# The opening of a four-layer kernel: order of the first loads, and a ternary rounding shared with GpSimd

## Chip, core and metric

One Trainium2 chip; the kernel runs on one of its cores. The metric is the device time of one execution in microseconds, here the median of three runs. Engines are named as the profile names them: PE (TensorE), DVE (VectorE), ACT (ScalarE), POOL (GpSimd), SP (SyncE).

## What is computed

Four conditioned layers one after the other on x of 64 sequences, 64 tokens and 256 features, in float32. Only the first is touched by the change, and only in its opening:

```python
def _L0_cond_ref(x, cond, norm_w, up_w, down_w):
    def act_quant(x):
        scale = 127.0 / jnp.clip(jnp.max(jnp.abs(x), axis=-1, keepdims=True), 1e-05, None)
        return jnp.clip(jnp.round(x * scale), -128.0, 127.0) / scale
    def weight_quant(w):
        scale = 1.0 / jnp.clip(jnp.mean(jnp.abs(w)), 1e-05, None)
        return jnp.clip(jnp.round(w * scale), -1.0, 1.0) / scale
    scale = cond @ norm_w.T + 1.0
    ms = jnp.mean(x * x, axis=-1, keepdims=True)
    h = x * (scale[:, None, :] * jax.lax.rsqrt(ms + EPS))
    u = h @ up_w.T
    val, gate = jnp.split(u, 2, axis=-1)
    h = val * jax.nn.gelu(gate, approximate=False)
    hq = h + jax.lax.stop_gradient(act_quant(h) - h)
    wq = down_w + jax.lax.stop_gradient(weight_quant(down_w) - down_w)
    return hq @ wq.T + x
```

The other layers are an attention block with a gated feed-forward part (L1), a layer norm (L2) and a bottleneck whose weights are generated per sequence (L3): `dWd = (h_lang @ Wdd.T + bdd) * 0.1`, and the like for `dWu`.

## The kernel before

The 4096 tokens are worked in 8 blocks of 512, a block in 4 tiles of 128 tokens. For layer 0 the function `l0` runs 32 tiles n. A tile's two `upper` halves multiply x, scaled by the condition and split in two fp32r parts (`xh`, `xl`), by the up weights, split likewise, in three passes (`mm3`, L83 to L85); ACT turns the gate into `g` with Gelu and the row scale `rs` (L433), DVE multiplies into `h` (L434). `quant` (L440 to L447) finds the row maximum on DVE, rounds `h` to `q`, and lets SP issue a transposing DMA to `qt`. `lower(n)`, some tiles later, multiplies `qt` by the ternary down weights `wq` (L459) and adds x.

The opening, before the loop, is written out by hand, and each engine keeps to its order there, SP too. Inside the loop PE, ACT, DVE and POOL keep to program order, while SP's order comes from a scheduler. All DMAs of a queue are issued in its order, and a DMA whose buffer or completion counter is not free holds up those behind it.

The up weights come in four pieces j of 512 columns, `ups[j]`, in the order of need: piece 2 (gate) and 0 (value) for the first half of the tiles, 3 (gate) and 1 (value) for the second. `load_up(j, queue, chunks)` (L321) loads one; `half_hi` (L327, ACT) casts it to the high part and `half_lo` (L330, DVE) subtracts for the low part. Pieces 2 and 0 come over ACT's queue, 3 and 1 over SP's. `prep_load(i)` (L361) loads a block of x feature-major (`xf`) and token-major (`xt`); for block 0 it loads only the first half of `xf`, and `rest_load` (L374) the other half, `xt` and pieces 3 and 1. `prep_parts` (L387) scales and splits x; `prep_scale` (L401) takes four square sums of `xt` on ACT (L219) and the root `rs` on POOL (L210, L212). `first((0, 1))` (L404) multiplies the first halves of tiles 0 and 1 chunk by chunk, in 24 products (L415), and does the Gelu later. `warm` (L465) issues transposes of the identity before the data is there.

The ternary rounding of the down weights `wd` (two tiles of 4 x 256 columns in one buffer of eight) is in three parts: `ternary_load`, `ternary` (two absolute sums on ACT, L346) and `ternary_rest` (L348), which, after tile 2, sums over partitions on PE, takes the reciprocal in `sb`, and rounds in three instructions a tile on DVE, L357 to L359.

A guard copy is a one-column POOL copy into a load's target that reads an earlier load's data; it holds the load until that data is there. Before, they stand at L339 (wd, until piece 3), L380 (piece 3, until `cwn`, the condition weights), L274 (the first four `gt`, until `xt`) and L134 (`cwt`, until `gl`). `gt` are tiles of the weight generator's matrix: `gen_load` (L266), `gen_make` (L278, the products L285), `gen_stage` (L289, ACT copies) and `gen_store` (L303); the first four are worked at tile 5. `cond_load` (L128) loads `vc`, `bo` and `cwt` for the other condition vectors, which are computed at tile 6.

Of the kernel before, what the change touches and what calls it, by code (L numbers as in the profile page):

```python
# [8 lines left out]
F32 = mybir.dt.float32  # L9
F32R = mybir.dt.float32r  # L10
BF16 = mybir.dt.bfloat16
AF = mybir.ActivationFunctionType
ALU = mybir.AluOpType
# [4 lines left out]
P = 128  # L18
NB = 64
L = 64  # L20
D = 256
NTOK = NB * L
T = 512
NBLK = NTOK // T
BB = T // L
# [4 lines left out]
MAGIC = 12582912.0  # L30


V_NORM, V_AG, V_AB, V_AA, V_FG, V_FB, V_FA, V_LIN = range(8)
# [3 lines left out]
def tile_kernel(ctx: ExitStack, tc, xT, x, condT, cw, upT, downT, qkvT, woT, ghT, outT_w,  # L37
                vecs, rows, g1, g2, gb, out):
    nc = tc.nc
# [12 lines left out]
    pools = {}  # L52
# [24 lines left out]
    def tok(ap, i):  # L77

        return ap[i * T:(i + 1) * T, :].rearrange("(t p) d -> p t d", p=P)
# [7 lines left out]
    def b3(ap):  # L87
        return ap.rearrange("p (b l) -> p b l", l=L)
# [23 lines left out]
    def bc(v, c, i, bs=slice(0, BB)):  # L112

        n = bs.stop - bs.start
        return cv[:, v, c, i * BB + bs.start:i * BB + bs.stop].unsqueeze(2).broadcast_to([P, n, L])
# [10 lines left out]
    crest = {}  # L126

    def cond_load():  # L128
        nc.sync.dma_start(out=vc, in_=vecs)
        bo = crest["bo"] = pools["a"].tile([NB, D], F32, name="bo")  # L130
        nc.sync.dma_start(out=bo, in_=rows[0:1, :].broadcast_to([NB, D]))

        cwt = crest["w"] = pools["kv"].tile([P, TT, 2, 8, 32], F32, tag="vb", bufs=2, name="cwt")[:, :2].rearrange("p a e h d -> p (a e) (h d)")
        nc.gpsimd.tensor_copy(cwt[:, 0, 0:1], gl[:, 0:1])  # L134
        nc.sync.dma_start(out=cwt[0:64], in_=cw[:, 1:5, :])
        nc.sync.dma_start(out=cwt[64:128, 0:3], in_=cw[:, 5:8, :])
# [173 lines left out]
    def l0(hooks):  # L310
# [10 lines left out]
        def load_up(j, queue, chunks=slice(0, 2)):  # L321
            if j not in ups:
                ups[j] = main.tile([P, 2, 512], F32, tag="x1", bufs=X1, name=f"upst{j}")
            queue.dma_start(out=ups[j][:, chunks],
                            in_=upT.rearrange("(c p) n -> p c n", p=P)[:, chunks, j * 512:(j + 1) * 512])
# [4 lines left out]
        def half_lo(j, c):  # L330
            js = slice(j * 512, (j + 1) * 512)
            nc.vector.tensor_tensor(up[1][:, c, js], ups[j][:, c], up[0][:, c, js].bitcast(F32), ALU.subtract)

        def ternary_load():
            wd = pools["kv"].tile([P, 8, D], F32, tag="kb", bufs=2, name="wd")
            til["wd"] = [wd[:, 4 * j:4 * j + 4] for j in range(2)]

            for j in range(2):
                nc.gpsimd.tensor_copy(wd[:, 4 * j, 0:1], ups[3][:, j, 0:1])  # L339
            for j in range(2):  # L340
                nc.sync.dma_start(out=til["wd"][j], in_=downT.rearrange("(f p) d -> p f d", p=P)[:, 4 * j:4 * j + 4, :])

        def ternary():
            for j in range(2):
                wj = main.tile([P, 4, D], F32, tag="xn", bufs=1, name=f"wj{j}")
                nc.scalar.activation(wj, til["wd"][j], AF.Abs, accum_out=sa[:, j:j + 1])  # L346

        def ternary_rest():  # L348
            wd, ones = til.pop("wd"), til.pop("ones")
            pb = bank("mm")  # L350
            nc.tensor.matmul(pb[:, 0:2], lhsT=ones, rhs=sa, start=True, stop=True)
            nc.vector.tensor_reduce(sb[:, 0:1], pb[:, 0:2], AX.X, ALU.add)
            nc.vector.tensor_scalar(sb[:, 1:2], sb[:, 0:1], 1.0 / (FF * D), 1e-5, ALU.mult, ALU.max)
            nc.vector.reciprocal(sb[:, 2:3], sb[:, 1:2])
            for j in range(2):
                wj = main.tile([P, 4, D], F32, tag="xn", bufs=1, name=f"wk{j}")
                nc.vector.tensor_scalar(wj, wd[j], sb[:, 2:3], MAGIC, ALU.mult, ALU.add)  # L357
                nc.vector.tensor_scalar(wj, wj, -MAGIC, 1.0, ALU.add, ALU.min)
                nc.vector.tensor_scalar(wq[:, 4 * j:4 * j + 4, :], wj, -1.0, None, ALU.max)  # L359

        def prep_load(i):  # L361
            xf = pool.tile([P, 2, T], F32, tag="xf", bufs=1, name=f"xf{i}")
            xt = None if i == 0 else block(f"xt{i}")
            xfs[i] = xf
            blk[i] = [xt, None, parts(f"l0_{i}"), None]
            src = xT.rearrange("(c p) t -> p c t", p=P)[:, :, i * T:(i + 1) * T]
            if i == 0:

                nc.sync.dma_start(out=xf[:, :, :T // 2], in_=src[:, :, :T // 2])
            else:  # L370
                nc.sync.dma_start(out=xf, in_=src)
                nc.sync.dma_start(out=xt, in_=tok(x, i))

        def rest_load():  # L374

            xf = xfs[0]
            ups[3] = main.tile([P, 2, 512], F32, tag="x1", bufs=X1, name="upst3")
            ups[1] = main.tile([P, 2, 512], F32, tag="x1", bufs=X1, name="upst1")
            xt = blk[0][0] = block("xt0")
            nc.gpsimd.tensor_copy(ups[3][0:64, 0, 0:1], cwn[:, 0:1])  # L380
            load_up(3, nc.sync)
            load_up(1, nc.sync)
            nc.sync.dma_start(out=xt, in_=tok(x, 0))
            nc.sync.dma_start(out=xf[:, :, T // 2:], in_=xT.rearrange("(c p) t -> p c t", p=P)[:, :, T // 2:T])
            nc.sync.dma_start(out=ct[64:128], in_=condT)

        def prep_parts(i, bs=slice(0, BB)):  # L387

            xf, hl = xfs[i], blk[i][2]
            ts = slice(bs.start * L, bs.stop * L)  # L390
            xss = []
            for c in range(2):
                xs = main.tile([P, T], F32, tag="xg", bufs=2, name=f"xs{i}_{c}_{bs.start}")[:, ts]
                nc.vector.tensor_tensor(b3(xs), b3(xf[:, c, ts]), bc(V_NORM, c, i, bs), ALU.mult)
                xss.append(xs)
            for c in range(2):
                yield
                nc.scalar.copy(hl[0][:, c, ts], xss[c])
                nc.vector.tensor_tensor(hl[1][:, c, ts], xss[c], hl[0][:, c, ts].bitcast(F32), ALU.subtract)

        def prep_scale(i):  # L401
            blk[i][1] = rms(blk[i][0], f"l0_{i}")
# [65 lines left out]
            for _ in range(n):  # L468
                nc.tensor.transpose(pb[:, :P], ident, ident)

        for c in range(2):
            load_up(2, nc.scalar, slice(c, c + 1))
        prep_load(0)
        til["ones"] = pool.tile([P, P], F32, name="ones")

        nc.scalar.activation(sa, nhalf[:, 0:2], AF.Gelu)
        nc.gpsimd.memset(til["ones"], 1.0)
        for c in range(2):
            load_up(0, nc.scalar, slice(c, c + 1))
        rest_load()  # L480
# [2 lines left out]
        cond_norm()  # L483
        warm(10)

        for c, _ in enumerate(prep_parts(0, slice(0, BB // 2))):
            if c == 1:
                half_hi(2, 1)
            half_lo(2, c)
        for c in range(2):  # L490
            half_hi(0, c)
            half_lo(0, c)
        first((0, 1))
        for j in (3, 1):
            for c in range(2):
                half_hi(j, c)
                half_lo(j, c)
        prep_scale(0)
        for _ in prep_parts(0, slice(BB // 2, BB)):
            pass  # L500
        upper(0, 0, "rest")
# [7 lines left out]
        for n in range(N + 2):  # L509
            if n < N:  # L510
                if n > 1:
                    upper(n, 0)
                if n == 0:
                    ternary_load()
                if n in visits:
                    for _ in range(4):
                        gen_make()
                        gen_stage()
                for _ in range(0 if n == 4 else 2 if n in visits and (n + 3 in visits or n == visits[-1]) else 1):
                    gen_load(blk[0][0][:, n, 0:1] if n < 4 else None)  # L520
                    gen_store()
                upper(n, 1)
                if n == 1:
                    ternary()
                    blk[0][3] = block("x1_0")
                if n == 2:
                    ternary_rest()
                if n % TT == 0 and n // TT + 1 < NBLK:
                    prep_load(n // TT + 1)
                if n % TT == 1 and n // TT + 1 < NBLK:  # L530
                    for _ in prep_parts(n // TT + 1):
                        pass
                if n % TT == 2 and n // TT + 1 < NBLK:
                    prep_scale(n // TT + 1)
            if n == N - 1:
                quant(n)
            for hook in hooks.get(n, ()):
                hook()
            if n < N - 1:
                quant(n)  # L540

            if n > 3:
                for k in range({4: 0, N + 1: N - 1}.get(n, n - 3), {N: N - 1, N + 1: N}.get(n, n - 2)):
                    lower(k)
# [695 lines left out]
```

## Time and profile before

| | |
|---|---|
| median of three runs | 763.72 us (763.22 to 764.21) |
| profiled execution | 762.64 us |
| its span, first to last instruction | 760.9 us |
| mean granted TensorE clock | 0.999 |
| DMA queues of SP, POOL: share of 16 engines | 49.1%, 11.2% |

The opening by stages, busy microseconds of each engine (from the view that cuts the span into stretches):

| stretch, us | PE | DVE | ACT | POOL | DMA, GB/s |
|---|---|---|---|---|---|
| 0 to 4 | 2.65 | 0.00 | 1.49 | 2.79 | 78 |
| 4 to 8 | 3.83 | 1.50 | 1.37 | 0.00 | 308 |
| 8 to 12 | 4.00 | 3.14 | 2.69 | 0.64 | 375 |
| 12 to 16 | 4.00 | 2.93 | 3.35 | 0.69 | 310 |
| 16 to 20 | 4.00 | 2.39 | 2.62 | 1.48 | 378 |
| 20 to 24 | 4.00 | 3.83 | 2.70 | 0.00 | 172 |
| 24 to 28 | 4.00 | 3.91 | 2.89 | 0.00 | 94 |
| 28 to 32 | 4.00 | 3.76 | 2.61 | 1.80 | 346 |
| 32 to 36 | 4.00 | 3.83 | 0.17 | 0.00 | 201 |
| 36 to 40 | 2.47 | 3.86 | 0.00 | 0.00 | 131 |
| 40 to 44 | 3.93 | 3.83 | 1.33 | 0.00 | 66 |
| 44 to 48 | 3.58 | 3.83 | 2.88 | 1.14 | 144 |

Times in the trace count from the span's start. A row of a timeline gives start and length in us, engine, line, operation, output and input tiles with their shapes, and in brackets the idle time before it and what ended it. A row of waits gives the engine and line that waited, what for, and us in total, times, longest. Matmuls are pipelined, so that a busy PE need not be at its peak.

### The profile page before, as it was taken

To read this page: it belongs to the slowest core of one execution; us is meant where nothing else is said; L and a number is where in the kernel's file an instruction comes from. 1 tells how busy PE (TensorE), PEld (TensorE's weight loads), DVE (VectorE), ACT (ScalarE), POOL (GpSimd) and SP (SyncE) were. 2 spreads that over 40 slices of the span, in tenths; PEclk is the share of its full clock that TensorE was granted. 3 is DMA by queue.
4 is the path that set the end of the run, shared out by engine and by line. 5 is a ranking of instruction groups with operands and counts; after the bars stand their busy time and mean duration, and the time that the engine had idled before them with its cause. 6 is when DMAs were issued, how large, how long until landed. Compare 5 with 4: busy or idle time off the path is not lost.

```text
span 760.9 us, 17434 instructions
## 1 busy us (share of the span) xinstructions
PE 747.0 (98%) x7036; PEld 616.1 (81%) x7036; DVE 548.1 (72%) x868; ACT 396.8 (52%) x820; POOL 340.9 (45%) x356
## 2 busy tenths in 40 slices
PE   9989999999999999999999999999999999999997
PEld 7856776676686878888888888888888888888886
DVE  4988867877687699898899876646555555555666
ACT  5444445435345577888887674535353434434242
POOL 2023123032225327666656417464646464545291
PEclk9999999999999999999999999999999999999999
DMA  8779997998975865454555137713170809080811
GB/s 286 217 153 227 316 310 159 334 260 187 300 232 117 185 168 141 117 154 112 154 151 126 48 109 184 162 39 102 47 176 28 196 3 220 1 194 2 234 44 57
DMA packets 117440, 118.87 MB, mean 156 GB/s; under 512 B 39616, under 2 KB 101184, under 8 KB 117360
## 3 DMA queue, kind: packets, MB, share of 16 engines
q1 hardware_dynamic: 109216, 91.29, 49.1%
q0 software_dynamic: 7488, 25.37, 11.2%
q8 instruction: 55, 0.90, 0.5%
q10 hardware_dynamic: 656, 1.11, 0.5%
q14 instruction: 25, 0.20, 0.1%
HBM read 71.41 MB, written 29.56 MB: 133 GB/s over the span
## 4 chain that ended last, share of the span: by engine, by line
PE 84%; DVE 8%; DMA 2%; issue 2%; ACT 2%; POOL 1%; SPq 0%; DVEq 0%; ACTq 0%; POOLq 0%
PE mm L83 10%; PE mm L85 9%; PE mm L84 9%; PE gh L83 7%; PE gh L84 7%; PE gh L85 7%; PE acc L83 4%; PE acc L85 4%; PE acc L84 4%; PE mm L285 4%; PE mm L459 3%; PE mm L662 2%; PE S L621 2%; PE mm L243 2%; PE mm L919 2%
## 5 line engine op out<-in xcount | busy, mean ns | idle before, releaser
L83 PE MATMUL mm<-up,xhl 128*128 128x512 f32 x248 | 101.2, 408 | 1.6 <-DVE h L434 1.6
L84 PE MATMUL mm<-up,xhl 128*128 128x512 f32 x248 | 97.9, 395 | 0.0
L85 PE MATMUL mm<-up,xll 128*128 128x512 f32 x248 | 97.9, 395 | 0.0
L83 PE MATMUL gh<-xhf,gh 128*128 128x512 f32 x244 | 97.2, 398 | 0.0
L768 DVE TENSOR_TENSOR sg<-gh,sg 128x512 f32<-128x512 f32 x61 | 42.0, 688 | 76.3 <-ACT sg L767 39.9
L84 PE MATMUL gh<-xlf,gh 128*128 128x512 f32 x244 | 96.9, 397 | 0.0
L85 PE MATMUL gh<-xhf,gh 128*128 128x512 f32 x244 | 96.8, 397 | 0.0
L433 ACT ACTIVATE g<-mm,rs_l 128x512 f32<-128x512 f32 x64 | 43.7, 688 | 89.2 <-PE mm L85 53.4
L796 DVE TENSOR_TENSOR hlo<-sg,hhi 128x512 fp32r<-128x512 f32 x59 | 55.9, 948 | 31.1 <-ACT hhi L795 30.2
L795 ACT CAST hhi<-sg 128x512 fp32r<-128x512 f32 x59 | 36.5, 619 | 74.5 <-DVE sg L768 73.6
L434 DVE SCALAR_TENSOR_TENSOR h<-mm,rs_l,g 128x512 f32<-128x512 f32 x64 | 46.9, 746 | 39.3 <-PE mm L85 34.0
L83 PE MATMUL acc<-wout,hhi 128*128 128x256 f32 x248 | 72.7, 293 | 0.0
L85 PE MATMUL acc<-wout,hlo 128*128 128x256 f32 x248 | 70.2, 283 | 1.1 <-DVE hlo L796 1.1
L247 POOL TENSOR_TENSOR xg<-xg,cv 128x512 f32<-128x512 f32 x32 | 35.3, 1112 | 78.7 <-DVE xg L246 74.7
L84 PE MATMUL acc<-wout,hhi 128*128 128x256 f32 x248 | 70.0, 282 | 0.0
L83 PEld LDWEIGHTS mm<-up,xhl 128*128 128x128 f32 x248 | 46.6, 188 | 18.4 <-DVE h L434 3.5
L85 PEld LDWEIGHTS mm<-up,xll 128*128 128x128 f32 x248 | 46.5, 188 | 11.4
L85 PEld LDWEIGHTS gh<-xhf,gh 128*128 128x128 f32 x244 | 46.1, 189 | 10.8
L84 PEld LDWEIGHTS mm<-up,xhl 128*128 128x128 f32 x248 | 46.6, 188 | 9.7
L84 PEld LDWEIGHTS gh<-xlf,gh 128*128 128x128 f32 x244 | 46.3, 190 | 8.1
L83 PEld LDWEIGHTS gh<-xhf,gh 128*128 128x128 f32 x244 | 46.3, 190 | 8.1
L767 ACT ACTIVATE sg<-gh 128x512 f32<-128x512 f32 x61 | 36.0, 589 | 28.4 <-PE gh L85 28.1
(208 smaller groups left out, 1916.5 us busy)
## 6 DMA issues: line engine op xcount, KB each, us to landing
gt<-in_g SPq DMA_DIRECT2D x32, 512.0 KB, 8.6
rows<-alphad SPq DMA_DIRECT2D x48, 256.0 KB, 4.3
vb<-vx SPq DMA_DIRECT2D x32, 256.0 KB, 4.7
wd<-s1d SPq DMA_DIRECT2D x32, 256.0 KB, 6.5
wu<-s2d SPq DMA_DIRECT2D x32, 256.0 KB, 6.1
xt<-in_x SPq DMA_DIRECT2D x8, 512.0 KB, 6.6
s1d<-stgs POOLq DMA_DIRECT2D x16, 256.0 KB, 9.7
s1d<-stg POOLq DMA_DIRECT2D x16, 256.0 KB, 9.4
```

Source lines behind the costliest of these rows:

```text
L83: nc.tensor.matmul(out, lhsT=l[0], rhs=r[0], start=first, stop=False)
L84: nc.tensor.matmul(out, lhsT=l[0], rhs=r[1], start=False, stop=False)
L85: nc.tensor.matmul(out, lhsT=l[1], rhs=r[0], start=False, stop=last)
L247: nc.gpsimd.tensor_tensor(b3(xg), b3(xg), bc(vb, c, i), ALU.add)
L285: nc.tensor.matmul(pb[s][c * 64:(c + 1) * 64], lhsT=gl[h], rhs=gt[h, c * GC:(c + 1) * GC], start=True, stop=True, tile_position=(64 * s, 6 ...
L433: nc.scalar.activation(g, pg, AF.Gelu, scale=rs[:, t:t + 1])
L434: nc.vector.scalar_tensor_tensor(h[:, ch * 512:(ch + 1) * 512], pv, rs[:, t:t + 1], g, ALU.mult, ALU.mult)
L459: nc.tensor.matmul(py[:, :D], lhsT=qt[:, f, :], rhs=wq[:, f, :], start=f == 0, stop=f == 7)
L767: nc.scalar.activation(sg, pg, AF.Silu)
L768: nc.vector.tensor_tensor(sg, pv, sg, ALU.mult)
L795: nc.scalar.copy(h_hi, sg)
L796: nc.vector.tensor_tensor(h_lo, sg, h_hi.bitcast(F32), ALU.subtract)
```

## The change

Loads. `xf`'s first half comes as two DMAs, one a chunk of 128 features. Piece 2's second chunk is issued behind ACT's table load instead of ahead of it. `vc` and `bo` get guard copies that read `gl`, so they leave the first loads and come with `cwt`. Piece 3's guard reads chunk 0 of `xf` instead of `cwn`. In `rest_load` `xt` is issued ahead of piece 1. The guards of `wd`, of the first four `gt` and a new one on block 1's `xt` read piece 1.

Work. The scaling and splitting of x's first half is written out chunk by chunk, with piece 2's subtractions between, so that chunk 0 does not wait for chunk 1. `prep_scale(0)` goes ahead of piece 1's casts. The ternary rounding is done in place, columns 0 to 4 of eight on DVE and 5 to 7 on POOL, three instructions on each.

In the built program PE's order is as before. On SP, `xt` of block 2 moves from behind the third `gt` up to a place right behind the rest of block 0's loads, ahead of `wd`; `vc`, `bo` and both `cwt` stand between the transposes of tiles 1 and 2, and the fourth `gt` moves behind the transpose of tile 2. On POOL the three roundings stand between the root of block 0 and that of block 1, and the guards of `vc`, `bo`, `cwt` and the fourth `gt` behind the latter. On ACT the four square sums of block 0 stand between the casts of piece 3 and of piece 1.

```diff
     def cond_load():
+        bo = crest["bo"] = pools["a"].tile([NB, D], F32, name="bo")
+        nc.gpsimd.tensor_copy(vc[:, 0, 0:1], gl[:, 0:1])
+        nc.gpsimd.tensor_copy(bo[:, 0:1], gl[0:NB, 0:1])
         nc.sync.dma_start(out=vc, in_=vecs)
-        bo = crest["bo"] = pools["a"].tile([NB, D], F32, name="bo")
         nc.sync.dma_start(out=bo, in_=rows[0:1, :].broadcast_to([NB, D]))
...
         def ternary_load():
...
             for j in range(2):
-                nc.gpsimd.tensor_copy(wd[:, 4 * j, 0:1], ups[3][:, j, 0:1])
+                nc.gpsimd.tensor_copy(wd[:, 4 * j, 0:1], ups[1][:, j, 0:1])
...
         def ternary_rest():
...
-            for j in range(2):
-                wj = main.tile([P, 4, D], F32, tag="xn", bufs=1, name=f"wk{j}")
-                nc.vector.tensor_scalar(wj, wd[j], sb[:, 2:3], MAGIC, ALU.mult, ALU.add)
-                nc.vector.tensor_scalar(wj, wj, -MAGIC, 1.0, ALU.add, ALU.min)
-                nc.vector.tensor_scalar(wq[:, 4 * j:4 * j + 4, :], wj, -1.0, None, ALU.max)
+            for fs, eng in ((slice(0, 5), nc.vector), (slice(5, 8), nc.gpsimd)):
+                wj = wd[:, fs]
+                eng.tensor_scalar(wj, wj, sb[:, 2:3], MAGIC, ALU.mult, ALU.add)
+                eng.tensor_scalar(wj, wj, -MAGIC, 1.0, ALU.add, ALU.min)
+                eng.tensor_scalar(wq[:, fs], wj, -1.0, None, ALU.max)
 
         def prep_load(i):
...
-                nc.sync.dma_start(out=xf[:, :, :T // 2], in_=src[:, :, :T // 2])
+                for c in range(2):
+                    nc.sync.dma_start(out=xf[:, c, :T // 2], in_=src[:, c, :T // 2])
             else:
                 nc.sync.dma_start(out=xf, in_=src)
+                if i == 1:
+                    nc.gpsimd.tensor_copy(xt[:, 0, 0:1], ups[1][:, 0, 0:1])
                 nc.sync.dma_start(out=xt, in_=tok(x, i))
 
         def rest_load():
...
-            nc.gpsimd.tensor_copy(ups[3][0:64, 0, 0:1], cwn[:, 0:1])
+            nc.gpsimd.tensor_copy(ups[3][:, 0, 0:1], xf[:, 0, 0:1])
             load_up(3, nc.sync)
+            nc.sync.dma_start(out=xt, in_=tok(x, 0))
             load_up(1, nc.sync)
-            nc.sync.dma_start(out=xt, in_=tok(x, 0))
...
-        for c in range(2):
-            load_up(2, nc.scalar, slice(c, c + 1))
+        load_up(2, nc.scalar, slice(0, 1))
         prep_load(0)
         til["ones"] = pool.tile([P, P], F32, name="ones")
 
         nc.scalar.activation(sa, nhalf[:, 0:2], AF.Gelu)
         nc.gpsimd.memset(til["ones"], 1.0)
+        load_up(2, nc.scalar, slice(1, 2))
...
-        for c, _ in enumerate(prep_parts(0, slice(0, BB // 2))):
-            if c == 1:
+        for c in range(2):
+            xs = main.tile([P, T], F32, tag="xg", bufs=2, name=f"xs0_{c}_0")[:, :T // 2]
+            (xh, xl), ts = blk[0][2], slice(0, T // 2)
+            nc.vector.tensor_tensor(b3(xs), b3(xfs[0][:, c, ts]), bc(V_NORM, c, 0, slice(0, BB // 2)), ALU.mult)
+            nc.scalar.copy(xh[:, c, ts], xs)
+            half_lo(2, c)
+            nc.vector.tensor_tensor(xl[:, c, ts], xs, xh[:, c, ts].bitcast(F32), ALU.subtract)
+            if c == 0:
                 half_hi(2, 1)
-            half_lo(2, c)
...
         for j in (3, 1):
+            if j == 1:
+                prep_scale(0)
             for c in range(2):
                 half_hi(j, c)
                 half_lo(j, c)
-        prep_scale(0)
...
-                    gen_load(blk[0][0][:, n, 0:1] if n < 4 else None)
+                    gen_load(ups[1][:, n % 2, n:n + 1] if n < 4 else None)
```

## What the change should do to the time

> **What bounds the kernel now.** I read the page's busy shares first, then the waits of TensorE, then the chain of waits in the opening, then the timelines of VectorE, GpSimd and SyncE there.
>
> ```profile
> PE 747.0 (98%) x7036; PEld 616.1 (81%) x7036; DVE 548.1 (72%) x868; ACT 396.8 (52%) x820; POOL 340.9 (45%) x356
> ...
> PE mm L83 <- DVE h L434: 1.6, 1, 1.6
> PE mm L285 <- DVE h L434: 0.4, 1, 0.4
> ```
>
> TensorE (PE) is busy 98% of the span. An edit pays only by what it takes out of PE's idle or stretched time, and what the opening saves stays saved, for PE sets the pace after it. Of its waits only two lie where the change reaches, both for VectorE's `h` (L434). The chain, in order of time (start, length, what), says why VectorE is late:
>
> ```profile
> 6.71 7.04 DMA xt<-in_x
> 13.77 0.52 ACT junkl L219 x2
> ...
> 16.27 1.30 POOL rs_l L212
> 17.59 0.70 ACT g L433
> 18.32 0.76 DVE h L434
> ...
> 31.87 0.77 DVE wk L357
> ...
> 43.75 0.76 DVE h L434
> 44.55 1.07 PE mm L285 x2
> ```
>
> Up to 17.6 us the first `g` waits for x token-major (landed 13.74) and its four square sums; from 18.3 to 45 VectorE works with hardly a gap, the six roundings of the down weights (31.87 to 36.24, when the next reduction starts) among it. At 40.07 PE has waited 1.6 us for `h` of tile 3, at 44.55 another 0.4 for `h` of tile 4; the ScalarE evictions behind that slow the weight-generation products too (32 of them from 43.06 to 48.42). From about 48 us PE leads. So **a microsecond that VectorE gains before 45 is a microsecond of the run; one that PE alone gains is lost again at 40.**
>
> **The change, part by part.**
>
> *x first in two chunks, two small loads moved away, piece 3 held.* The first products cannot start much earlier: in PE's queue the ten warm-up transposes stand ahead of them.
>
> ```profile
> 5.15 2.39 PE L469 MATMUL mm<-ident 128*128 128x128 f32 x10
> ```
>
> They end at 7.54; the first product started at 7.71. The start gains at most 0.17 us, the chunks arriving sooner inside that block perhaps 0.3 more, and PE reaches the end of the first 24 products at about 13.2 instead of 13.7. That is PE time alone: worth nothing by itself. Holding piece 3 until chunk 0 has landed (it is half of a load that landed at 6.69, issued at 1.37 with a first small load there at 3.3: between 4.5 and 6.7, I take 5.6), plus a 0.18 us GpSimd copy, issues it near 5.9 instead of 3.47. It costs nothing as long as pieces 2 and 0 on ScalarE's queue still fill the engines: the DMA rates of the view of the first 50 us stay above 330 GB/s from 5 to 12.5 us, so piece 3 only takes its later place.
>
> *x token-major ahead of piece 1.* Landings before: piece 3 10.93, piece 1 12.20, xt 13.74, rest of x 14.45. The gaps are 1.27 us for piece 1 and 1.54 for xt. Without the 71 KB of the two small loads piece 3 lands at about 10.7; then xt 10.7+1.5 = 12.15, piece 1 13.45, rest of x 14.15. But ScalarE's order now is: casts of piece 3, four square sums, casts of piece 1, casts of x's second half, `g`. Square sums take 13.77 to 15.91 = 2.15 us, so they end at 14.3 and the two casts (1.15) at 15.45. VectorE subtracts the second half of piece 1 only then (0.69), multiplies x twice (0.76), ScalarE casts twice (0.70): `g` at about 17.5 against 17.59. The 1.6 us by which xt is early are eaten by what now stands behind the sums; **gain 0.1 us**. Ends: xt at 12.5 loses 0.2, xt at 11.7 gains 0.5. PE now waits about 1 us for piece 1 near 14 to 16 and ends tile 0 at 16.6 (before 16.5); its 1.6 us of waiting at 38.5 covers that.
>
> *Rounding split 5 : 3.* VectorE's six instructions (754, 694, 694 ns, twice) become three of 1280 elements. From 128x256 at 345 ns (L236) and 128x1024 at 694 comes 0.45 ns an element: 870+810+810 = 2.49 us. Alone that would end at 34.4, 1.9 us earlier. GpSimd runs three of 768 elements at the same time, and here a trace row decides. Timelines of GpSimd, then VectorE, in a later stage:
>
> ```profile
> 231.06 1.57 POOL L227 TENSOR_TENSOR xla<-xg,xha 128x512 fp32r<-128x512 f32 x1 [0.73 <-ACT xha L226]
> ...
> 230.75 0.75 DVE L443 TENSOR_SCALAR h<-h,am 128x1024 f32<-128x1024 f32 x1
> 231.54 1.65 DVE L445 TENSOR_SCALAR q<-h 128x1024 bf16<-128x1024 f32 x1
> ```
>
> L445 alone takes 0.69. It stood until 232.50 behind GpSimd's instruction, which had itself waited for L443's end at 231.50. The two engines take turns, an instruction at a time. The Trainium skill's "SBUF — State Buffer" (the part on the two physically separate sides) states it as a rule: VectorE in a two-port mode and GpSimd hold a shared port pair exclusively, for a whole instruction. By that rule alone GpSimd's full length P stands between VectorE's instructions. The row says a little less: the hold was 1.00 us of an instruction that takes 1.28 alone, as 0.28 of dispatch hid behind the wait. So VectorE's stretch is 2.49 plus two holds of P - 0.28 (the third falls beside the next reduction, L440, which such neighbours did not stretch elsewhere).
>
> P is not in the trace. From below: a memset of 2048 elements reads nothing and takes 1.80 us; with 0.19 fixed (L210, four elements) that is 0.79 ns an element, P = 0.80. From above: two-input L227, 1.28 for 512, P = 1.83. One input lies between; I take 1.0 because the skill's "GPSIMD Engine Reference" (engine selection) calls one-input work roughly line rate, which lies near the memset. Then holds are 0.72: 31.87+2.49+1.44 = 35.80, and the reduction starts at 35.75 instead of 36.24: **gain 0.5**. By the rule (holds of 1.0) the reduction would start at 36.31 and 0.1 would be lost. With the row's holds P = 0.80 gains 0.9, P = 1.83 loses 1.15. Lower(0) reaches PE at 36.6 and needs GpSimd's last part at about 36.55: no cost at this P.
>
> *What queues behind GpSimd's share.* Block 1's root (L210, L212; inputs ready at 29.5) and the guard copies for vc, bo, cwt and the fourth gt stand behind it. The root is ready near 38.05 (its end yields to L443, as at 155.8 us, where it took 1.55) and is wanted at 40.13 less the gain: covered. The guards wait for L445 and end at 38.8 to 39.15. **SyncE** now has, in this order: vc, bo, two cwt, tile 2's transpose, the fourth gt. Before:
>
> ```profile
> 31.37 0.48 SPq L135 DMA_DIRECT2D cwt<-in_cw  x1
> 31.90 1.31 SPq L447 DMA_TRANSPOSE qt<-q  x1
> 33.27 0.58 SPq L136 DMA_DIRECT2D cwt<-in_cw  x1
> 33.95 0.54 SPq L275 DMA_DIRECT2D gt<-in_g  x1
> ```
>
> After: 38.9 + 0.46+0.49+0.48+0.58+0.1 of gaps = 41.0 for the transpose, +1.25 = 42.3 for gt, landing 4.4 to 4.8 later (rows of the third and fourth gt) at 46.7 to 47.1. The fourth generation product began at about 47.4 and is now wanted at 46.8: **cost 0 to 0.3, taken as 0.1**. It also caps what VectorE may gain unless GpSimd is done sooner.
>
> *Other moved loads.* Block 2's xt goes up from 27.0 to about 11 us (SyncE waits there only for piece 0's last subtraction, done by 11). It adds 512 KB ahead of wd, issued near 14.0 and 14.5 instead of 11.5 and 12.0. With landings of 4.4 and 5.4 they are there at 18.4 and 19.9; ScalarE wants them at 20.41 and 21.58. Block 1's x feature-major is issued near 17 instead of 15.3 and lands at 22.5; wanted at 24.37. Its cover would cost, if gone, the same microsecond for microsecond on VectorE.
>
> Sum: -0.1 - 0.5 + 0.1 = **-0.5 us**. The profiled execution took 762.64 (span 760.9 and 1.74 around it), so it would take 762.1; it lay 1.1 below the median of 763.72 (763.22 to 764.21). Median: **763.2 us**. A change of this kernel under 0.2%, 1.53 us, is not told from none.
>
> **Rivals.**
> 1. *The engines do not collide on these instructions*: VectorE gains 1.9, the root and guards are 2 us earlier, gt lands before 45 and is no cap. With the 0.1: 761.7. For: only two-input GpSimd work is seen to hold VectorE. Against: L210, one input, itself took 0.53 at 29.58, waiting for L445's end.
> 2. *xt's early landing passes through*: were piece 1 cast before the sums end, `g` would start near 16 and 1.5 us come on top of the 0.5 less a late gt: 762.0. Against: the order above has one answer unless everything lands earlier too.
> 3. *Slower: GpSimd's rounding is as dear as its two-input work*, P = 1.83. VectorE's stretch ends 1.15 later; GpSimd ends at 39.0, lower(0) waits 2.4 us; guards at 41, transpose 43.1, gt issued at 44.4, landed at 49.0 against 47.4: +1.6, or 765.3. It decides from P about 1.25, where VectorE gains nothing; gt alone costs from P about 1.0.
> 4. *Neither*: holds and gt eat the gain, P between 1.15 and 1.5: 763.7 to 764.6.
>
> **How the numbers follow.** Forecast 0.45, rival 4 0.23, rival 1 0.11, rival 2 0.08, rival 3 0.13. Rivals 1 and 2 end beyond -1.53: faster 0.19 together. Rival 3 lies about the upper bound; with what I have not seen in its favour it counts as slower: 0.13. Rest 0.68. The range runs from rival 1 to rival 3's lower side, 761.6 to 765.2.
>
> **What would show it.** Right: first `g` at 17.4 to 17.7 although xt lands near 12.1; L357's three VectorE instructions show two of about 1.5 us; PE's wait for `h` near 40 falls from 1.6 to about 1.0; the fourth gt lands near 47. Wrong: `g` before 17.0, roundings of 0.87 and 0.81 beside GpSimd's, or PE waiting for gt or for wq.

## The result, and the profile after

The changed kernel took 766.92 us (median of six runs, 765.87 to 768.21) against 763.47 for the kernel before beside it: ratio 1.004, 95% interval 1.0026 to 1.0054. A second series (below) gave 1.003 (1.0013 to 1.0047). It is slower by some 2.3 to 3.1 us, and the forecast of 763.2 was wrong. The profiled execution took 766.26 us, with a span of 764.5.

The page's first part, and from the view of TensorE's waits the rows for `gt`, `wq` and `h` of the opening; the first two are new, the third stands as before (there L285):

```profile
PE 747.8 (98%) x7036; PEld 617.0 (81%) x7036; DVE 548.8 (72%) x865; ACT 396.8 (52%) x820; POOL 347.0 (45%) x362
```

```profile
PE mm L287 <- DMA gt<-in_g: 1.5, 1, 1.5
...
PE mm L465 <- POOL wq L362: 1.3, 1, 1.3
...
PE mm L287 <- DVE h L440: 0.4, 1, 0.4
```

TensorE's wait of 1.6 us for `h` of tile 3 is gone. In its place stand 1.3 us for `wq`, whose last writer is now GpSimd (L362), and 1.5 us for the fourth `gt`, at the end of the weight generation. The wait for `wq` fills the slot of the old wait; the wait for `gt` is new time. The chain of waits that leads to the wait for `gt`, in order of time (start, length, what):

```profile
17.70 0.69 ACT g L439
...
31.98 0.90 DVE wd L360
32.90 1.44 DVE wd L361
34.36 1.32 DVE wq L362
35.69 1.14 DVE am L446
37.24 1.22 DVE h L449
...
44.72 4.63 DMA gt<-in_g
49.48 1.09 PE mm L287 x8
```

Before, the chain here ran through VectorE until `h` of tile 4 at 43.75 and straight into the generation products at 44.55. Now a DMA of 4.63 us, issued at 44.72, stands in it. The next product of the up weights starts at 50.50 instead of 48.42: 2.1 us lost in the opening. The two profiled spans differ by 3.6 us; the other 1.5 lie later in the run (see e5).

Why the DMA is issued so late is read through two queues, each of which works in order. GpSimd's timeline:

```profile
32.11 1.54 POOL L360 TENSOR_SCALAR wd<-wd,sb 128x768 f32<-128x768 f32 x1 [15.82 <-DVE sb L356]
33.73 3.26 POOL L361 TENSOR_SCALAR wd<-wd 128x768 f32<-128x768 f32 x1
37.07 2.15 POOL L362 TENSOR_SCALAR wq<-wd 128x768 bf16<-128x768 f32 x1
...
41.26 0.18 POOL L276 COPY gt<-upst 128x1 f32<-128x1 f32 x1
```

and SyncE's:

```profile
41.12 0.34 SPq L132 DMA_DIRECT2D vc<-in_vecs  x1
...
43.36 1.27 SPq L453 DMA_TRANSPOSE qt<-q  x1
44.72 0.53 SPq L277 DMA_DIRECT2D gt<-in_g  x1
```

The three roundings were to end at 36.55 and ended at 39.22. Behind them in GpSimd's queue stand block 1's root and the guards; the guards release the loads of `vc`, `bo` and `cwt` on SyncE, behind which the transpose and `gt` stand. From there on every event is late by nearly as much against the forecast: the guards by 2.3 us, the transpose by 2.4, `gt` by 2.4.

VectorE's timeline beside it, and two rows of before (L443 and L445 are now L449 and L451):

```profile
32.90 1.43 DVE L361 TENSOR_SCALAR wd<-wd 128x1280 f32<-128x1280 f32 x1
34.36 1.32 DVE L362 TENSOR_SCALAR wq<-wd 128x1280 bf16<-128x1280 f32 x1
...
37.24 1.20 DVE L449 TENSOR_SCALAR h<-h,am 128x1024 f32<-128x1024 f32 x1
38.48 1.29 DVE L451 TENSOR_SCALAR q<-h 128x1024 bf16<-128x1024 f32 x1
```

```profile
37.87 0.76 DVE L443 TENSOR_SCALAR h<-h,am 128x1024 f32<-128x1024 f32 x1
38.66 0.69 DVE L445 TENSOR_SCALAR q<-h 128x1024 bf16<-128x1024 f32 x1
```

VectorE's next reduction starts at 35.61, 0.63 sooner than before (0.74 counted from the reciprocal in `sb`; 0.5 was forecast). But then L449 takes 1.20 instead of 0.76 and L451 1.29 instead of 0.69, beside GpSimd's third instruction: 1.04 us go, and `h` of tile 3 starts at 39.69, 0.42 later than before.

### The profile page after: what moved, and what is told of

Its sections match the earlier page's. It is cut to its first block, busy times and chain, and to the rows that moved or that the text cites. A ratio compares the mean times of both kernels' runs of the same rounds, so it can differ in the third digit from the quotient of the medians.

```text
span 764.5 us, 17439 instructions
## 1 busy us (share of the span) xinstructions
PE 747.8 (98%) x7036; PEld 617.0 (81%) x7036; DVE 548.8 (72%) x865; ACT 396.8 (52%) x820; POOL 347.0 (45%) x362
## 4 chain that ended last, share of the span: by engine, by line
PE 81%; DVE 9%; DMA 4%; issue 2%; ACT 1%; POOL 1%; SPq 0%; DVEq 0%; ACTq 0%; POOLq 0%
PE mm L83 9%; PE mm L85 9%; PE mm L84 9%; PE gh L83 7%; PE gh L85 7%; PE gh L84 7%; PE acc L83 4%; PE acc L85 4%; PE acc L84 4%; PE mm L465 3%; PE mm L287 3%; DMA x2d<-ax 2%; PE S L633 2%; PE mm L674 2%; PE mm L931 2%
## 5 line engine op out<-in xcount | busy, mean ns | idle before, releaser
L83 PE MATMUL mm<-up,xhl 128*128 128x512 f32 x248 | 101.3, 409 | 0.0
L83 PE MATMUL gh<-xhf,gh 128*128 128x512 f32 x244 | 97.3, 399 | 0.0
L807 ACT CAST hhi<-sg 128x512 fp32r<-128x512 f32 x59 | 36.5, 619 | 74.5 <-DVE sg L780 73.6
L83 PE MATMUL acc<-wout,hhi 128*128 128x256 f32 x248 | 72.8, 294 | 0.0
L83 PEld LDWEIGHTS mm<-up,xhl 128*128 128x128 f32 x248 | 46.7, 188 | 16.6 <-issue 2.4
L83 PEld LDWEIGHTS gh<-xhf,gh 128*128 128x128 f32 x244 | 46.3, 190 | 8.0
```

The lines of the kernel that those rows point to most:

```text
L83: nc.tensor.matmul(out, lhsT=l[0], rhs=r[0], start=first, stop=False)
L807: nc.scalar.copy(h_hi, sg)
```

## The experiments

Two theories stood at the start. **A**: GpSimd's share makes the loss. **B**: the moved loads do. The time at which the opening reaches the rounding moves from profile to profile (column "sb" below: 30.96 to 32.96 in the six kernels whose loads are those of before), and a kernel's runs spread by 3 us or more. So I read two numbers for each kernel: the ratio of the times, and in its profile the **stretch** from the start of the reciprocal in `sb` (31.67 before) to the first L83 product behind the weight generation (48.42): 16.75 us before, 18.72 after. Column "us" is the ratio to the kernel before, less 1, times 763.5 us, with its 95% interval; columns "sb", "tile 3's h" and "L83" are starts in the one profiled execution.

| kernel | sb | tile 3's h | L83 | stretch | against 16.75 | us by ratio |
|---|---|---|---|---|---|---|
| before | 31.67 | 39.27 | 48.42 | 16.75 | | |
| after | 31.78 | 39.69 | 50.50 | 18.72 | +1.97 | +3.1 (2.0 to 4.1) |
| e5, after again | 32.54 | 40.44 | 51.70 | 19.16 | +2.41 | +2.3 (1.0 to 3.6) |
| e1, loads only | 31.43 | 38.90 | 48.05 | 16.62 | -0.13 | +0.5 (-0.4 to 1.4) |
| e2, split only | 30.96 | 38.87 | 48.65 | 17.69 | +0.94 | +1.5 (0.6 to 2.4) |
| e3, share behind guards | 32.36 | 40.27 | 49.40 | 17.04 | +0.29 | +1.1 (0.5 to 1.8) |
| e6, gt early | 31.88 | 39.78 | 48.91 | 17.03 | +0.28 | +0.4 (-0.5 to 1.2) |
| e4, share of one eighth | 32.19 | 38.98 | 48.12 | 15.93 | -0.82 | -0.2 (-0.9 to 0.6) |
| e12, share without min, max | 31.43 | 38.31 | 47.46 | 16.03 | -0.72 | -0.6 (-1.4 to 0.2) |
| e10, loads, piece 1 first | 32.74 | 40.23 | 49.37 | 16.63 | -0.12 | +0.9 (0.2 to 1.6) |
| e11, one eighth, no loads | 31.45 | 38.24 | 47.39 | 15.94 | -0.81 | -1.3 (-2.1 to -0.5) |
| e13, three instructions | 31.60 | 38.55 | 47.69 | 16.09 | -0.66 | -1.0 (-1.5 to -0.5) |
| e7, ScalarE's share | 31.26 | 37.28 | 47.07 | 15.81 | -0.94 | -1.5 (-2.2 to -0.7) |
| e14, the same in two | 32.96 | 38.66 | 48.45 | 15.49 | -1.26 | -1.1 (-1.9 to -0.4) |

### Loads or share (e1, e2)

e1 keeps the whole change but the share; e2 puts the share alone into the kernel before.

```diff
-            for fs, eng in ((slice(0, 5), nc.vector), (slice(5, 8), nc.gpsimd)):
+            for fs, eng in ((slice(0, 4), nc.vector), (slice(4, 8), nc.vector)):
```

> The whole change except GpSimd's share: VectorE does all six roundings (two halves, in place). Theory A (GpSimd's share makes the loss: its instructions and VectorE's take turns, wq and the guards behind it come late, and with them the transpose and gt): 763.2 to 763.8, ratio within 0.1% of before; h of tile 3's next scaling starts at 39.2 to 39.5, no wait of PE for wq or gt, first matmul of L83 after the generation at 48.3 to 48.7. Theory B (the moved loads make it: token-major x early, slower DMA in the first 12 us, another order of the loads in the queues): 765.5 to 767, L83 again at 50 or later.

> The kernel before with the 5:3 split of the rounding alone; no load is moved. Theory A: 765 to 767, with the last GpSimd rounding ended at 38.8 to 39.4, PE waiting 1 to 1.5 for wq, and gt landed at 48.5 to 49.5. Theory B: 762.7 to 763.7 (VectorE's 0.5 gained, and nothing lost).

e1's stretch is that of before, and its time is not told from that of before. e2 is slower by 1.5 us; its last GpSimd rounding ended at 38.40, and PE waited 1.4 for `wq`. Its time fits neither forecast: PE never waits for `gt` in e2. There are no `vc` and `bo` in its queue, and the scheduler put `gt` ahead of the transpose, so that it was issued at 41.52. The 0.94 us of its stretch are 0.31 of VectorE and a wait of 0.6 of L83 for `x` (L460), the last step of `lower`. Theory A holds; the loss of the whole change needs share and loads together, because only together do they put `gt` so late.

### The queue behind the share (e3, e6)

e3 issues GpSimd's three roundings behind block 1's root and the guards. e6 leaves them in their place and loads the fourth `gt` right behind the third, near 26 us, so that it depends on nothing behind the roundings.

```diff
-            for fs, eng in ((slice(0, 5), nc.vector), (slice(5, 8), nc.gpsimd)):
+            def share(fs, eng):
...
+            share(slice(0, 5), nc.vector)
+            til["share"] = lambda: share(slice(5, 8), nc.gpsimd)
...
+                if n == 3:
+                    til.pop("share")()
```

```diff
-                for _ in range(0 if n == 4 else 2 if n in visits and (n + 3 in visits or n == visits[-1]) else 1):
+                for _ in range(0 if n in (3, 4) else 2 if n == 2 or n in visits and (n + 3 in visits or n == visits[-1]) else 1):
```

> The changed kernel, with GpSimd's three roundings issued behind block 1's root and the guards of the vectors and of gt instead of ahead of them. Theory A in two parts: the queue part goes (transpose of block 1 near 41, gt landed by 47.2, no wait for gt), the wait for wq stays (lower of tile 0 delayed 1.3 to 2.5): 763.8 to 765.2. If the queue were no part of it (turn-taking alone): 766 to 767. Theory B: 766 to 767 as well, with gt early and L83 after the generation early, the loss later on.

> The changed kernel, with the fourth gt loaded beside the third near 22 us, so that neither its guard behind GpSimd's roundings nor its place behind tile 2's transpose on SP counts. If the queue and the late gt cost 1.5 of the 2.1 us: first matmul of L83 after the generation at 48.8 to 49.2, ratio to before 1.0005 to 1.0015. If the generation is late for VectorE's sake (its h held by GpSimd), it stays at 50 or later, ratio near 1.003.

Both give the same stretch, 17.03 and 17.04. TensorE's timeline of e6:

```profile
39.37 1.36 PE L465 MATMUL mm<-wq,qt 128*128 128x256 bf16 x11 [1.30 <-POOL wq L362]
43.56 1.09 PE L287 MATMUL mm<-gt,gl 64*64 64x512 f32 x8
45.05 3.94 PE L287 MATMUL mm<-gt,gl 64*64 64x512 f32 x24 [0.40 <-DVE h L440]
```

The wait for `wq` is still there, 1.30 us long; the products of the generation run through without a wait for `gt`. So of the changed kernel's 1.97 us in the stretch, 1.7 are the late `gt`, and 0.3 are VectorE's (from `sb` to `h` of tile 3: 7.90 us against 7.60). The wait for `wq` costs nothing: it lies where PE would have waited for `h` anyway.

### Once more, the whole change (e5)

> The changed kernel once more, on the chip of the next two. If all its loss lies in the opening, as share_last (1.0 us late after the generation, 1.15 slower) makes likely: ratio 1.0025 to 1.0035 (about 2.1 us late there, 1.9 to 2.7 slower). If the later 1.5 us of its first profile (the waits for ax between 260 and 430 us) come with the change: 1.004 or more, and those waits again between 2 and 3 us.

The ratio is 1.003, and TensorE waits 1.9 us for `gt`. Its waits for `ax`, a tile of a later layer, between 260 and 430 us are there again: 2.2 us, 2.4 in the first profile of the changed kernel, 0.8 before. But in e11 and e13, which move no load and are faster than before, they are 2.6 and 2.5. So they need not come from the change. Over all profiles they are 1.2 to 3.1 us in the eight kernels with the moved loads and 0.2 to 2.6 in the six without; whether the loads have a part in them is open.

### A smaller share (e4, e11)

```diff
-            for fs, eng in ((slice(0, 5), nc.vector), (slice(5, 8), nc.gpsimd)):
+            for fs, eng in ((slice(0, 7), nc.vector), (slice(7, 8), nc.gpsimd)):
```

e4 does it in the changed kernel, e11 in the kernel before.

> The changed kernel with a share of one eighth (256 columns) for GpSimd instead of three eighths. Theory A: GpSimd's last rounding ends by 36.5 to 37, no wait for wq, guards back at 38.5 to 39, gt not waited for: 763 to 764.2. Theory B: 766 to 767, as in the changed kernel.

> The kernel before with a share of one eighth for GpSimd, no load moved. The changed kernel with this share gained 0.8 us between sb and h of tile 3 (6.8 instead of 7.6) but began 0.5 late. Without the loads: h of tile 3 at 38.4 to 38.6, L83 after the generation at 47.5 to 47.8, ratio 0.9985 to 0.9995. If a share behind the root costs more than VectorE gains: 1.000 to 1.001.

Both did better than expected. With 256 columns GpSimd is done at 37.2 (e4) and 36.5 (e11), nothing waits for `wq` or `gt`, and the stretch is 0.8 us shorter than before. VectorE's second and third instruction, of 1792 elements, took 1.26 and 1.16; alone they would take about 1.10 (worked out from 0.69 for 1024 and 1.23 for 2048 elements, e13), so they lost 0.16 and 0.06 beside GpSimd's.

### How long GpSimd's instructions are (e8, e9)

e8 adds the three instructions on scratch data beside the first loads. e9 puts them, and two more, ahead of all of VectorE's work; from its edit:

```diff
...
+    nc.vector.memset(scr, 0.5)
+    for k in (3, 1):
+        sk = scr[:, :k]
+        nc.gpsimd.tensor_scalar(sk, sk, nhalf[:, 0:1], MAGIC, ALU.mult, ALU.add)
+        nc.gpsimd.tensor_scalar(sk, sk, -MAGIC, 1.0, ALU.add, ALU.min)
+        nc.gpsimd.tensor_scalar(scb[:, :k], sk, -1.0, None, ALU.max)
+        nc.gpsimd.tensor_scalar(sk, sk, -1.0, None, ALU.max)
+        nc.gpsimd.tensor_scalar(sk, sk, -1.0, MAGIC, ALU.mult, ALU.add)
```

> The kernel before, with the three roundings on GpSimd added over scratch data between 3.4 and 8 us, for 768 and then for 256 columns, where VectorE has little to do: the length of one without a neighbour. The prediction took 1.0 us for 768 columns (0.80 and 1.83 its ends). Holds of 0.62 and 0.51 us of VectorE in the changed kernel's profile say 0.8 to 0.95; rival 3 said 1.83.

> The kernel before, with GpSimd's instructions over scratch data put ahead of everything that VectorE's first work waits for, so that VectorE is idle beside all but the first: for 768 and then 256 columns scale and add, add and min, max to bf16, max to fp32, scale and add by constants. Theory turns (each is about 0.9 us, and VectorE's instructions slip in between parts of it): 0.85 to 1.0 for all of 768 columns. Theory slow (the instructions with min and max take long by themselves and hold VectorE only for a part): scale and add 0.9, add and min 2.5 to 2.8, max to bf16 1.5 to 2.2.

e8 gave 0.90 for the first, and 2.80 and 2.28 for the others, although VectorE worked for only 0.7 us beside the second. Until then I had read the 3.26 and 2.15 of the changed kernel as instructions of about 0.9 that VectorE interrupts several times (theory turns). The other reading is that they are long by themselves (theory slow). e9 tells the two apart. GpSimd's timeline of e9; the rows are, in order, the five instructions of the diff for 768 columns:

```profile
2.12 0.91 POOL L104 TENSOR_SCALAR scr<-scr,nhalf 128x768 f32<-128x768 f32 x1 [1.29 <-DVE scr L101]
3.11 2.81 POOL L105 TENSOR_SCALAR scr<-scr 128x768 f32<-128x768 f32 x1
6.00 2.15 POOL L106 TENSOR_SCALAR scb<-scr 128x768 bf16<-128x768 f32 x1
8.23 2.13 POOL L107 TENSOR_SCALAR scr<-scr 128x768 f32<-128x768 f32 x1
10.44 0.84 POOL L108 TENSOR_SCALAR scr<-scr 128x768 f32<-128x768 f32 x1
```

VectorE is idle all this time. Multiply and add take 0.84 to 0.91, near the 1.0 that the prediction took for all three; with a `min` or a `max` in it an instruction takes 2.1 to 2.8. It isn't the bf16 output (2.15 against 2.13). For 256 columns the same five took 0.48, 1.08, 0.85, 0.84 and 0.41. Theory turns falls, and theory slow holds.

### The decisive one: the same share without min and max (e12)

e12 is the changed kernel with multiply and add in GpSimd's second and third instruction. It leaves out the clamp to -1 and 1 for GpSimd's three eighths of the weights, so its output is not the layer's.

```diff
...
+                else:
+                    eng.tensor_scalar(wj, wj, 1.0, -MAGIC, ALU.mult, ALU.add)
+                    eng.tensor_scalar(wq[:, fs], wj, 1.0, 0.0, ALU.mult, ALU.add)
```

> The changed kernel, every queue in the same order; on GpSimd's share alone the second and third rounding become multiply and add (1.0 and the constant, then 1.0 and 0), so the clamp to -1 and 1 is left out for that three eighths of the weights. If what failed in the prediction is the length of GpSimd's min and max (2.81 and 2.15 alone instead of 1.0): GpSimd ends near 37, PE waits less than 0.3 for wq, gt is issued near 42.5 and not waited for, L83 after the generation at 48.3 to 48.8, ratio 0.9995 to 1.0010, what the prediction gave. If any share of this size, or its place in the queue, costs this: ratio 1.0025 to 1.004.

GpSimd's timeline of e12:

```profile
31.75 1.54 POOL L360 TENSOR_SCALAR wd<-wd,sb 128x768 f32<-128x768 f32 x1 [15.72 <-DVE sb L356]
33.38 1.30 POOL L365 TENSOR_SCALAR wd<-wd 128x768 f32<-128x768 f32 x1
34.76 1.28 POOL L366 TENSOR_SCALAR wq<-wd 128x768 bf16<-128x768 f32 x1
```

and VectorE's:

```profile
32.54 1.43 DVE L362 TENSOR_SCALAR wd<-wd 128x1280 f32<-128x1280 f32 x1
34.01 1.34 DVE L363 TENSOR_SCALAR wq<-wd 128x1280 bf16<-128x1280 f32 x1
35.27 1.20 DVE L450 TENSOR_REDUCE am<-h 128x1 f32<-128x1024 f32 x1
```

GpSimd ends at 36.04, no wait for `wq`, `gt` issued at 41.33 and not waited for, ratio 0.9992 (0.9982 to 1.0002). Two of VectorE's instructions are held, the third of GpSimd's lies beside the reduction and costs nothing. This is the picture that the prediction drew, with every queue in the changed kernel's order and an end somewhat better than it said (the stretch is 0.7 us shorter than before); only the operations of two instructions, and with them their length, differ from the changed kernel. That length is the cause.

### The order of piece 1 (e10)

e10 is e1 with piece 1 ahead of `xt` again.

```diff
-            nc.sync.dma_start(out=xt, in_=tok(x, 0))
             load_up(1, nc.sync)
+            nc.sync.dma_start(out=xt, in_=tok(x, 0))
```

> The kernel of loads_only with piece 1 ahead of x token-major again (one part of the change undone). If the later piece 1 costs what loads_only lost at the opening: piece 1 lands at 12.7 to 13.2, no wait of PE for up near 15, but first g not earlier than 17.5, time 762.6 to 763.6. If x token-major early is worth its 0.1 to 0.3 us: 763.6 to 764.

No wait of PE for piece 1 was expected. Piece 1 had landed by 12.24, yet PE waits 1.2 us for its cast. On ScalarE the square sums stand ahead of that cast now and wait for `xt` until 13.69; the cast starts at 15.73. The order of the work holds it, not the order of the loads. The kernel is 0.9 us slower than before, and not told from e1.

### Versions without GpSimd (e13, e7, e14)

e13 joins VectorE's six roundings into three of 2048 elements. e7 clamps before it rounds, which gives the same values because -1 and 1 are whole numbers, and leaves the last step to ScalarE, idle there; from its edit:

```diff
...
-                nc.vector.tensor_scalar(wj, wd[j], sb[:, 2:3], MAGIC, ALU.mult, ALU.add)
-                nc.vector.tensor_scalar(wj, wj, -MAGIC, 1.0, ALU.add, ALU.min)
-                nc.vector.tensor_scalar(wq[:, 4 * j:4 * j + 4, :], wj, -1.0, None, ALU.max)
+                nc.vector.tensor_scalar(wj, wd[j], sb[:, 2:3], 1.0, ALU.mult, ALU.min)
+                nc.vector.tensor_scalar(wj, wj, -1.0, MAGIC, ALU.max, ALU.add)
...
+            til["last"] = lambda: [nc.scalar.activation(wq[:, 4 * j:4 * j + 4, :], wd[j], AF.Copy, bias=-MAGIC) for j in range(2)]
```

(`last` is called behind block 1's square sums.) e14 is e7 with VectorE's part in two instructions of 2048.

> The kernel before, with the six roundings of VectorE joined into three of 2048 elements, nothing on GpSimd. From 754 ns for 1024 and 890 for 1280 elements one takes about 1.3: the stretch is 3.85 instead of 4.37, h of tile 3 at 38.75, ratio 0.999 to 0.9997. If split_7_1's gain of 0.8 is GpSimd's doing rather than that of fewer instructions, ratio here 1.000.

> The kernel before, with the rounding in another form: VectorE scales and clamps to -1 and 1 and adds the rounding constant in two instructions a half, ScalarE (idle from 32 to 40 us) takes the constant off and writes bf16. No GpSimd, no load is moved. If VectorE's time before 45 us is worth its full length in the run: two instructions of 0.69 and two gaps less, h of tile 3 at 37.8 instead of 39.27, PE's wait of 1.6 for it down to 0.1 to 0.3, time 761.3 to 761.9 (ratio 0.998 to 0.9988). If something else is late next (gt, the transposes), 762.3 to 763.

> act_round with VectorE's part in two instructions of 2048 elements instead of four of 1024 (ScalarE's stays in two halves). VectorE gains 0.3 more than in act_round; but wq's first half comes 0.6 later, near 35.2, and its second near 36.2, about where PE wants it. 761.3 to 762 (ratio 0.9975 to 0.9985) if that still fits; 762 to 763 if PE waits for wq.

All three are faster than before. e13 gets 0.65 us of VectorE's time back (`sb` to `h` of tile 3: 6.95 us against 7.60) with no other engine at all, so most of e11's 0.81 comes from fewer instructions and not from GpSimd: three of 2048 elements took 1.28, 1.23 and 1.23 us, where six of 1024 took 0.75, 0.69 and 0.69 each time. e7 gets 1.58 back (6.02), and its time falls by 1.5 us: 0.9981 (0.9971 to 0.9991), the best of the study beside e11. In the stretch only 0.94 of it is left: L83 now waits 0.6 us for VectorE's `x` (L460), the last step of `lower`. e14 has the shortest stretch, 15.49, but is not told from e7 (0.9985, 0.9975 to 0.9995): PE now waits 1.5 us for `g`, which stands behind the two ScalarE roundings; the wait that was thought possible was one for `wq`.

## Why the prediction was wrong, step by step

- **Rounding on GpSimd, P = 1.0 for each of the three**: this is the step that failed. The first measured 0.91 alone, the second 2.81, the third 2.15. The prediction asked how many inputs an instruction reads, and took the nearest rows that it had (a memset, which reads nothing, with the fixed part of the four-element L210). No instruction of GpSimd in the kernel before has a `min` or a `max`, and these set the length. The Trainium skill's "GPSIMD Engine Reference" (engine selection) calls one-input work roughly line rate; here the other two take 2.5 to 3 times as long as multiply and add. The upper end of 1.83, read from two-input work, was too low as well.
- **Holds of P - 0.28 = 0.72, two of them**: near in size, but in part by luck. From 694 ns for 1024 and 1.23 us for 2048 elements (e13), one of 1280 takes 0.83 alone (an estimate); 1.43 and 1.32 mean holds of 0.60 and 0.49. The first stood beside GpSimd's multiply and add, for which P - 0.28 with the measured 0.91 gives 0.63. The second stood beside the add and `min`; with its 2.81 the formula gives 2.53, so there the picture of turns by whole instructions failed, in the prediction's favour. The reduction gained 0.63 where 0.49 was forecast.
- **The third falls beside the next reduction**: failed as a consequence. L362 on GpSimd started at 37.07 (34.76 in e12), and so beside L449 and L451, which lost 0.44 and 0.60. VectorE's gain of 0.5 became a loss of 0.3.
- **The queue behind the share, cost 0 to 0.3, taken as 0.1**: the chain was right to its members (root, guards, `vc`, `bo`, two `cwt`, transpose, `gt`, 4.4 to 4.8 us to land; measured 4.63), but it was made to start 2.7 us too early, at 36.55 instead of 39.22. It cost 1.7 us: by the prediction's own sum `gt` had no slack left, so that most of the delay reached PE.
- **Lower(0) needs wq at 36.55, no cost**: wq came at 39.22 and PE waited 1.3, but the cost is nothing all the same, as e6 shows: the wait replaced that for `h`.
- **xt ahead of piece 1, gain 0.1**: the first `g` started at 17.70 instead of 17.5 (17.59 before), and two misses lie behind the small difference. First, xt landed at 12.69, not at 12.15. x's first chunk landed at 6.25, not at 5.6, and so piece 3 was issued at 6.51 instead of near 5.9; and the DMA engines did not stay as full as the prediction took them to be: they moved 269 GB/s from 4 to 8 us and 295 from 8 to 12, where before it was 308 and 375. How much each of the two adds is not shown. Second, from the end of the square sums to `g` it took 2.85 us, where the parts that the prediction lists add up to 3.3. That the order on ScalarE eats xt's lead was right. In the eight profiles with the moved loads `sb` starts at 32.04 on average, in the six without at 31.65; the groups spread by 1.3 and 2.0 us. e1's +0.5 (-0.4 to 1.4) would fit a cost of some tenths, but does not show one.
- **Start and moved loads, nothing**: the first 24 products ended no sooner (L83 follows them at 14.13, before at 13.93; 13.2 was forecast), and as forecast this cost nothing that is seen. Nothing was seen of block 2's early `xt` either; e1's stretch is that of before.

The terms as measured: VectorE +0.3 for -0.5, `gt` +1.7 for +0.1, the first loads +0.1 to 0.5 for -0.1 (the 0.5 from e1, not told from noise), together +2.1 to 2.5, where the two series gave +3.1 (2.0 to 4.1) and +2.3 (1.0 to 3.6). Rival 3 had the right picture of the queues to within 0.4 us (guards 41, transpose 43.1, `gt` issued 44.4 and landed at 49.0; measured 41.1 to 41.4, 43.36, 44.72 and 49.35), but for a wrong reason: not two-input cost but the operation makes the instructions long. Its VectorE price of 1.15 didn't come true, because the long instructions hold VectorE for only part of their length.

## What to carry to other kernels

Price an instruction on GpSimd by its operations, not only by its inputs and elements: find a row with the same operations, or measure one on scratch data where nothing runs beside it. When work moves to an engine, follow the copies and guards that stand behind it in its queue to the DMA that they release, and ask which of these has no slack. Before a busy engine's work is shared, try fewer and longer instructions, and an engine that stands idle at that place (here ScalarE): that gave 1.0 (e13) and 1.5 us (e7), where the change with its share of three eighths lost 2.3 to 3.1.

## What the runs showed of the hardware

- GpSimd's `tensor_scalar` on 128x768 float32 alone: 0.84 to 0.91 us with multiply and add, 2.13 with one `max`, 2.81 with add and `min` (e9). Why is open.
- A long GpSimd instruction does not hold VectorE for its whole length. In the changed kernel the third rounding took 2.15 us (37.07 to 39.22), no longer than alone, and in this time VectorE's L449 began and ended (37.24 to 38.44, 0.44 longer than before) and L451 began; L451 ended at 39.77, 0.60 longer than before. The prediction weighed the rule of the Trainium skill's "SBUF — State Buffer" (the two physically separate sides), a hold for the full instruction: for multiply and add (e12) the holds of 0.60 and 0.5 are 0.3 below the instruction's length, as in the row that the prediction used; for `min` and `max` the rule would have cost VectorE 2.81 and 2.15, and the changed kernel shows 0.49 and 1.04.
